# One more step between copy and use: at the projection, at a batch's turned inputs and at the router's counts

## The chip, the cores and the metric

The kernel runs on one core of one Trainium2 chip. The time is device microseconds (us) from start to end of one execution. A run's time is a median over executions; the profile is one further execution, recorded by the hardware profiler. TensorE (PE) multiplies matrices, VectorE (DVE) and ScalarE (ACT) work on elements, GpSimd (POOL) does elementwise work and indirect transfers, and SyncE (SP) issues most of the DMA transfers. Each engine, and SP's queue of transfers, takes its instructions strictly in the order in which the program wrote them: an instruction that waits holds up everything behind it on that engine.

## The reference

Input is x of shape (8, 256, 128) in float32: 8 batches of 256 tokens with 128 features. Four blocks follow each other, each with a residual and a layer normalisation:

```
x = LN(x + attention(x))      # 8 heads; a query sees its last 64 keys and 32 more,
                              # picked by an indexer's scores (top_k of 96)
x = LN(x + experts(x))        # 8 experts, each token goes to the best one, gelu
x = LN(x + recurrence(x))     # gated linear recurrence with 16 states per feature
x = LN(x + moe(x))            # sigmoid encoder, 8 experts, the best two are mixed
```

The part that matters here is the first block and the routing of the second. The indexer computes `relu(q_i k_i)` summed over 4 index heads and picks 32 past keys per query beside its own window. The keys and values of the picked positions are gathered, the 8 heads' softmax is taken over 96 keys, and the output is projected. The router takes the argmax of 8 sigmoids.

## The kernel before, in words

**Groups.** Attention is done in 128 groups (b, f, g): batch b of 8, half f of 2, and g of 8. The main loop (lines 1232 to 1265) goes through them as n = 16b + 8f + g. In iteration n the program writes the scores of group n (L710, L716 on PE, L725 on DVE), the turning of group n-2 (L746, copied by ACT in L751), the value product of group n-3 (L761), the exponentials of n (L731 on ACT), then a tick, then the reciprocal and the weights of n (L736 on DVE, L738 on ACT), then a second tick. This text calls the first tick of an iteration A and the second B. All of a group's own matmuls lie ahead of A; nothing of the groups on PE lies between A and B of one iteration.

**Sides.** Everything else is a generator in the list `sides`. At each tick every side runs from one `yield` to the next (a step), in the order in which the sides were added. So a `yield` moves all that follows in its generator by one tick, and changes whether it is written at an A or at a B. The sides here are:

- `picked(k)` (L444): the indexer of batch k, added at n = 16k - 22. Step 1 transposes x on PE through `transposed_steps` (L370), step 2 copies it on ACT (L378), step 3 has the matmuls L453 to L458, step 4 copies them out on ACT, step 6 makes the table `tab` (L478 to L480 on DVE), steps 9 to 12 find the 32 best (L519 to L523) and cast their numbers to bytes (L528, DVE), step 13 stores them to DRAM (`list`, L530, on SP's queue), and step 14 reads them back spread over the partitions (`idxb`, L535, on SP's queue). After that it does the same for the later queries (steps 14 to 22).
- `gathered(k)` (L549), in two parts: part A is added by step 14 of `picked(k)`, part B by step 22. Its first step writes the first one-hot `hot` on POOL (L560, from `idxb`); two steps later come the gathering matmuls `pgm` (L572) from that `hot`, then `pgl` a step later. POOL adds the turned keys (L589). How far a part may go is held back by the groups that still read the key buffers (L599).
- `asked(b)` (L617) makes the queries; `as_weights` (L675) copies them with 12 transfers on SP's queue (4 of L678, 8 of L680). `as_weights(b, 1)` is called at the top of iteration n = 16b + 1, ahead of its scores and its ticks.
- `projected(b, f)` (L769), added when group (b, f, 7) has had its value product, at n = 16b + 8f + 10. Step 1 transposes on DVE, step 3 on PE (L781), step 4 copies `olT` on ACT (L784), step 6 multiplies (L789). For f = 1 it goes on with the normalisation and with `routed0(b)` (L808), whose input goes through `transposed_steps` too: router matmul L817 in step 13, the one-hot of the best expert (`first_best`, L799) in step 15, the counting matmuls L835 and L836 in step 17, and in step 18 the places and two indirect transfers that POOL issues (L851).
- `response()` (L1125) computes the recurrence's response on POOL (L1150, L1168) and DVE (L1149, L1158, L1171), one POOL product every three or four ticks.
- `experts(0)` (L916) follows `routed0(5)` in the same generator; `gated(b)` (L1090), which also calls `transposed_steps`, comes after the main loop.

Which ticks these steps fall on follows from the code by counting: step s of a side that was added in iteration n0 is written at A of n0 + (s-1)/2 where s is odd, and at B of n0 + (s-2)/2 where s is even. For `picked(k)` step 14 is B of iteration 16k - 16, that is B of 16(k-1); the next thing that the program writes on SP's queue is `as_weights(k-1, 1)` at the top of iteration 16(k-1) + 1.

Of the kernel before, what the change touches and what calls it, by code (L numbers as in the profile page):

```python
# [104 lines left out]
def tile_two_layers(ctx: ExitStack, tc: tile.TileContext, a: dict, out: bass.AP):  # L105
# [8 lines left out]
    def ps(tag, name):  # L114
        return psum.tile([P, 512], F32, tag=tag, name=name, bufs={"e": 1, "x": 3}.get(tag))
# [254 lines left out]
    def transposed_steps(src, name, tag="x", copy=None):  # L370

        n = src.shape[1]
        pt = ps(tag, name + "_ps")
        for f in range(n):
            nc.tensor.transpose(pt[:, f * P : (f + 1) * P], src[:, f, :], ident)
        yield
        t = work.tile([P, 2 * P], F32, tag=f"xT{n}", name=name, bufs=4)
        (copy or nc.scalar.copy)(t[:, : n * P], pt[:, : n * P])  # L378
        yield
        return t  # L380

# [26 lines left out]
    def normalised_steps(dst, src, n, tag):  # L408

        mv = moments(src, n, tag)  # L410
        yield
        rs = work.tile([P, n], F32, tag=tag + "_rs", name=tag + "_rs")
        nc.scalar.activation(rs, mv[:, :, 1], AF.Ln, bias=eps)
        nc.scalar.activation(rs, rs, AF.Exp, scale=-0.5)
        yield
        for f in range(n):
            nc.vector.tensor_scalar(dst[:, f, :], src[:, f, :], mv[:, f, 0:1], rs[:, f : f + 1], ALU.subtract, ALU.mult)
        yield
# [25 lines left out]
    def picked(b, st):  # L444


        xb = x[:, 2 * b : 2 * b + 2, :]
        xT = yield from transposed_steps(xb, f"xT_{b}", copy=None if b else nc.vector.tensor_copy)


# [318 lines left out]
    def projected(b, f, st):  # L769

        if f == 0:
            st["x1p"] = work.tile([P, 2, D], F32, tag="x1p", name=f"x1p_{b}")
        x1p, po = st["x1p"], st["po"]

        olt = work.tile([P, NH, CKV], F32, tag="olt", name=f"olt_{b}_{f}")
        nc.vector.transpose(out=olt, in_=po[:, : TB0 * 8].rearrange("p (t h) -> p h t", h=NH))
        yield
        yield
        pt = ps("x", f"polT_{b}_{f}")
        for k in range(2):  # L780
            nc.tensor.transpose(pt[:, k * P : (k + 1) * P], olt[:, 4 * k : 4 * (k + 1), :].rearrange("p h c -> p (h c)"), ident)  # L781
        yield
        olT = work.tile([P, 2, P], F32, tag="olT", name=f"olT_{b}_{f}")
        nc.scalar.copy(olT.rearrange("p k t -> p (k t)"), pt[:, : 2 * P])  # L784
        yield
        yield
        pp = ps("o", f"pproj_{b}_{f}")
        for k in range(2):
            nc.tensor.matmul(pp[:, :D], olT[:, k, :], wuvo[:, k, :], start=k == 0, stop=k == 1)  # L789
        yield  # L790
        nc.vector.tensor_add(x1p[:, f, :], pp[:, :D], x[:, 2 * b + f, :])
        if f:
            yield
            yield from normalised_steps(x[:, 2 * b : 2 * b + 2, :], x1p, 2, "ln1")
            st["normed"] = True
            yield from routed0(b)


    def first_best(dst, val, n, top, tag):  # L799

        nc.vector.tensor_reduce(top, val, AX.X, ALU.max)
        nc.vector.tensor_tensor(dst, val, top.unsqueeze(2).to_broadcast([P, n, 8]), ALU.is_equal)
        nc.vector.tensor_mul(dst, dst, first8.unsqueeze(1).to_broadcast([P, n, 8]))
        lead = work.tile([P, n], F32, tag=tag + "_lead", name=tag + "_lead")
        nc.vector.tensor_reduce(lead, dst, AX.X, ALU.max)
        nc.vector.tensor_tensor(dst, dst, lead.unsqueeze(2).to_broadcast([P, n, 8]), ALU.is_equal)

    def routed0(b):  # L808


        k = next(k for k, (b0, nb) in enumerate(GROUPS) if b0 <= b < b0 + nb)
        ts = slice(2 * b, 2 * b + 2)
        x1T = yield from transposed_steps(x[:, ts, :], f"x1T_{b}")
        pr = ps("x", f"prt_{b}")
        for f in range(2):
            fs = slice(f * E0, (f + 1) * E0)
            nc.tensor.matmul(pr[:, fs], x1T[:, f * P : (f + 1) * P], wr, start=True, stop=True)  # L817
        yield
        rt = work.tile([P, 2, E0], F32, tag="rt", name=f"rt_{b}")
        rtf = rt.rearrange("p f e -> p (f e)")  # L820
        nc.vector.tensor_tensor(
            rt, pr[:, : 2 * E0].rearrange("p (f e) -> p f e", e=E0), br.unsqueeze(1).to_broadcast([P, 2, E0]), ALU.add
        )
        nc.scalar.activation(rtf, rtf, AF.Exp, scale=-1.0)
        yield
        nc.vector.tensor_scalar_add(rtf, rtf, 1.0)
        route = work.tile([P, 2, E0], F32, tag="route", name=f"route_{b}")
        nc.vector.reciprocal(route, rt)
        oh = onehot[:, ts, :]
        first_best(oh, route, 2, best_prob[:, ts], "moe0")  # L830
        yield
        yield
        ohf = oh.rearrange("p t e -> p (t e)")
        pc = ps("x", f"pcount_{b}")
        nc.tensor.matmul(pc[:, : 2 * E0], before, ohf, start=True, stop=True)  # L835
        nc.tensor.matmul(pc[:, 2 * E0 : 4 * E0], every, ohf, start=True, stop=True)  # L836
        yield
        rank, cnt = (pc[:, u * 2 * E0 : (u + 1) * 2 * E0].rearrange("p (t e) -> p t e", e=E0) for u in range(2))
        base, at = bases[k], work.tile([P, 2, E0], F32, tag="mat", name=f"mat_{b}")
        nc.vector.tensor_add(at[:, 0, :], base, rank[:, 0, :])  # L840
        nc.vector.tensor_add(base, base, cnt[:, 0, :])
        nc.vector.tensor_add(at[:, 1, :], base, rank[:, 1, :])
        nc.vector.tensor_add(base, base, cnt[:, 1, :])
        nc.vector.tensor_mul(at, at, oh)
        nc.vector.tensor_reduce(place[:, ts], at, AX.X, ALU.add)
        nc.vector.tensor_copy(places[:, ts], place[:, ts])  # L846
        while k not in clear:
            yield
        for f in range(2):
            t = 2 * b + f  # L850
            nc.gpsimd.indirect_dma_start(  # L851
                out=sorted_in[k][:], out_offset=bass.IndirectOffsetOnAxis(ap=places[:, t : t + 1], axis=0),
                in_=x[:, t, :], in_offset=None,
            )
        state[b]["placed"] = True
        yield
# [233 lines left out]
    def gated(b):  # L1090
        xb = x[:, 2 * b : 2 * b + 2, :]
        tag = "x" if b == B - 1 else tags["gate"]
        x2T = yield from transposed_steps(xb, f"x2T_{b}", tag=tag)
        pg = ps(tag, f"pg_{b}")
        for f in range(2):
# [136 lines left out]
    for n in range(len(groups) + 3):  # L1232
# [19 lines left out]
        if third:  # L1252
            third.latents()
            if third.g == 7:
                then = [experts(k) for k, (b0, nb) in enumerate(GROUPS) if (b0 + nb - 1, 1) == (third.b, third.f)]
                ending = chain(projected(third.b, third.f, state[third.b]), *then)
                if n < len(groups) + 2:
                    sides.append((ending, 1))
# [466 lines left out]
```

## Time and profile before

| | |
|---|---|
| median of 3 runs | 852.54 us (850.76 to 854.84) |
| the profiled execution, its own time | 855.22 us |
| its span, first to last instruction | 853.5 us |
| mean granted TensorE clock | 0.816 |
| busy: PE, DVE, POOL, ACT | 641.5, 482.9, 360.0, 324.6 us |
| groups of attention (n = 0 to 127) | from about 45 to about 617 us |
| part with the second layer's tail | from about 700 to 853 us |

A line of the timeline gives the start and the length in us, the engine, the line of the code, the operation, what it writes and reads, and how many instructions were merged; in brackets stands how long the engine sat idle before it and what ended that. SPq is SP's queue of transfers. A line of the waits gives the waiting engine and line, what it waited for, the total in us, how often, and the longest.

### The profile page before, as it was taken

Reading aid. Unit: us, or ns where it says so; the run is one execution under the profiler, and the core shown is the slowest. Engines: PE = TensorE matmul, PEld = TensorE weight load, DVE = VectorE, ACT = ScalarE, POOL = GpSimd, SP = SyncE. Lnnn points to the kernel's source line nnn. Section 1 sums busy time; section 2 is a strip of 40 time slices with the busy share of each in tenths; the row PEclk is TensorE's granted clock in tenths of the full one; section 3 lists DMA queues with packets and bytes.
Section 4 is the critical chain, followed back from the end, with each engine's and each line's share of the span. In section 5 each row is a group of like instructions: output and inputs, shape, how many; then the busy total and the mean of one; then the engine's idle time right before and its main releaser. Section 6 shows DMA issues by size and latency. Waiting matters only on the chain.

```text
span 853.5 us, 26479 instructions
## 1 busy us (share of the span) xinstructions
PE 641.5 (75%) x11019; PEld 418.8 (49%) x11019; DVE 482.9 (57%) x1792; ACT 324.6 (38%) x955; POOL 360.0 (42%) x222
## 2 busy tenths in 40 slices
PE   4477768885888897877898878787727839687973
PEld 3143434562554564454565454586616726344541
DVE  4766845679767664667665673222154345456673
ACT  3332432442343354254354444557522323322422
POOL 1454668559647735756618436000031240211110
PEclk9997677667857767898879987989877959898787
DMA  5232364210201101101101215448996540022220
GB/s 192 65 82 61 94 184 140 86 38 2 61 7 33 37 27 38 37 27 46 37 27 42 59 34 144 125 130 222 253 191 187 171 71 3 2 100 100 113 112 25
DMA packets 96192, 72.64 MB, mean 85 GB/s; under 512 B 21864, under 2 KB 86952, under 8 KB 95048
## 3 DMA queue, kind: packets, MB, share of 16 engines
q1 hardware_dynamic: 94200, 68.42, 29.3%
q0 software_dynamic: 1024, 2.10, 0.9%
q8 instruction: 87, 1.43, 0.7%
q10 hardware_dynamic: 848, 0.43, 0.2%
q14 instruction: 33, 0.27, 0.1%
HBM read 49.14 MB, written 13.91 MB: 74 GB/s over the span
## 4 chain that ended last, share of the span: by engine, by line
PE 37%; DVE 30%; ACT 12%; DMA 8%; issue 5%; POOL 4%; SPq 4%; POOLq 0%; DVEq 0%; ACTq 0%
PE pgm L572 4%; PE pe L746 4%; PE s L716 3%; PE s L710 3%; DVE cur L510 3%; PE py L1001 3%; PE pgl L572 3%; ACT sm L731 3%; PE pqr L647 2%; PE ph L986 2%; DVE hg L1608 2%; DMA w<-in_L_ffn_W_dram 2%; POOL hot L560 2%; PE pqi L453 2%; ACT eT L751 1%
## 5 line engine op out<-in xcount | busy, mean ns | idle before, releaser
L560 POOL TENSOR_SCALAR hot<-idxb,masks 128x1024 f32<-128x1024 uint8 (+2 forms) x64 | 182.1, 2851 | 107.0 <-DMA idxb<-list 65.1
L751 ACT COPY eT<-pe 128x256 f32<-128x256 f32 x128 | 47.1, 368 | 159.7 <-PE pe L746 159.3
L725 DVE CUSTOM_DVE_ANT_0 sm<-s,allowed 128x128 f32<-128x128 f32 x128 | 40.4, 316 | 114.0 <-PE s L716 104.9
L572 PE MATMUL pgm<-hot,tab 128*32 128x256 f32 (+2 forms) x1024 | 88.4, 462 | 19.3 <-POOL hot L560 18.4
L738 ACT ACTIVATE en<-sm,stat 128x128 f32<-128x128 f32 x128 | 51.4, 401 | 89.9 <-DVE stat L736 86.6
L731 ACT ACTIVATE sm<-sm,stat 128x128 f32<-128x128 f32 x128 | 51.6, 403 | 72.5 <-DVE stat L725 63.4
L851 POOL DMA_INDIRECT sorted_in<-x,places x16 | 16.3, 1017 | 125.1 <-DVE places L846 48.8
L746 PE MATMUL pe<-eye,en 128*32 128x128 f32 x1024 | 62.6, 324 | 4.5 <-ACT eT L751 4.5
L710 PE MATMUL s<-kst,qw 64*32 64x96 f32 x1024 | 58.3, 305 | 8.6 <-DVE qw L688 8.6
L572 PE MATMUL pgl<-hot,tab 128*32 128x256 f32 (+2 forms) x512 | 47.7, 460 | 20.1 <-DVE gtmp L580 8.3
L746 PE MATMUL pe<-eyes,en 128*32 128x128 f32 x1024 | 62.7, 325 | 0.0
L1467 POOL TENSOR_TENSOR ln_rs<-ln_rs,minus_half 128x4 f32<-128x4 f32 x16 | 16.3, 1020 | 104.2 <-DVE ln_rs L1466 73.9
L716 PE MATMUL s<-kg,qbd 128*32 128x32 f32 x2048 | 57.1, 236 | 0.0
L572 PEld LDWEIGHTS pgm<-hot,tab 128*32 128x32 f32 (+2 forms) x1024 | 26.9, 123 | 60.2 <-issue 29.6
L710 PEld LDWEIGHTS s<-kst,qw 64*32 64x32 f32 x1024 | 28.2, 141 | 51.6 <-issue 39.6
L716 PEld LDWEIGHTS s<-kg,qbd 128*32 128x32 f32 x2048 | 41.7, 147 | 22.8 <-issue 13.7
L589 POOL TENSOR_TENSOR kg<-gtmp 128x256 f32<-128x256 f32 x48 | 35.8, 749 | 30.6 <-DVE gtmp L580 27.9
L588 DVE STREAM_TRANSPOSE rows<-pgl 128x256 f32<-128x256 f32 x48 | 21.5, 447 | 47.3 <-ACT kg L587 47.3
L580 DVE TENSOR_TENSOR gtmp<-pgm,cg 128x512 f32<-128x512 f32 x48 | 32.4, 676 | 19.8 <-PE pgm L572 19.7
L1001 PE MATMUL py<-w,hT 128*128 128x128 f32 x240 | 35.6, 309 | 10.1 <-ACT hT L992 7.9
L736 DVE RECIPROCAL stat<-stat 128x1 f32<-128x1 f32 x128 | 19.4, 152 | 39.5 <-ACT sm L731 38.0
L761 PEld LDWEIGHTS pav<-eT,win 96*32 96x32 f32 x1024 | 37.7, 134 | 2.9 <-issue 0.8
(298 smaller groups left out, 1490.4 us busy)
## 6 DMA issues: line engine op xcount, KB each, us to landing
w<-in_L_ffn_W_dram SPq DMA_DIRECT2D x60, 256.0 KB
sorted_in<-zero SPq DMA_DIRECT2D x34, 256.0 KB
toep<-kpad SPq DMA_DIRECT2D x32, 256.0 KB
gb<-gates SPq DMA_DIRECT2D x8, 1024.0 KB
idxb<-list SPq DMA_DIRECT2D x16, 256.0 KB
qbd<-qd SPq DMA_DIRECT2D x60, 64.0 KB
qw<-qd SPq DMA_DIRECT2D x120, 32.0 KB
mxs<-sorted_in SPq DMA_DIRECT2D x30, 64.0 KB
```

Of the source, the lines that this page charges most:

```text
L560: nc.gpsimd.tensor_scalar(out=t[:m].rearrange("p j g k -> p j (g k)"), in0=st["listed", u][:m].rearrange("p (j g) k -> p j g k", j=2)[:, : ...
L572: nc.tensor.matmul(pt[DR * i : DR * (i + 1), :], tab[:m, k, c, :], t[:m, :, i, :], start=k == 0, stop=k == len(hot) - 1,)
L589: nc.gpsimd.tensor_tensor(kgf[:, 0], t1[:, 0], t1[:, 1], ALU.add)
L710: nc.tensor.matmul(s[TB0 * j : TB0 * (j + 1), :WIN], qws[f][:, :, :, 8 * j + g].rearrange("p i h -> p (i h)"), st["kst"][:, TB0 * w : TB0 ...
L716: nc.tensor.matmul(s[TB0 * j : TB0 * (j + 1), WIN:KEYS], qbds[f][:, k, :, :, 8 * j + g].rearrange("p i h -> p (i h)"), kg[:, 1 - k, :], st ...
L725: nc.vector.tensor_tensor_reduce(out=self.sm, in0=s[:, :KEYS], in1=allowed[f][:, g * KEYS : (g + 1) * KEYS], scale=-SCALE, scalar=3.0e38, ...
L731: nc.scalar.activation(self.sm, self.sm, AF.Exp, bias=self.stat[:, 0:1], scale=-1.0, accum_out=self.stat[:, 1:2])
L738: nc.scalar.activation(self.en, self.sm, AF.Copy, scale=self.stat[:, 2:3])
L746: nc.tensor.matmul(pe[rows, k * P : (k + 1) * P], self.en[:, WIN:KEYS] if k else self.en[:, rows], own_rows[i] if k else ident, start=True ...
L751: nc.scalar.copy(self.eT.rearrange("p k t -> p (k t)"), pe[:, 0 : 2 * P])
L761: nc.tensor.matmul(st["po"][js, TB0 * g : TB0 * (g + 1)], rows if k else st["win"][:, w, :], self.eT[: P if k else WIN, k, js], start=k == ...
L1001: nc.tensor.matmul(py[:, u * D : (u + 1) * D], hT[u][:, c, :], w2[:, c, :], start=c == 0, stop=c == FFN0 // P - 1)
```

## The change

Three `yield`s are added, and nothing else: no instruction is added or removed.

```diff
@@ transposed_steps (called by picked, routed0 and gated) @@
         (copy or nc.scalar.copy)(t[:, : n * P], pt[:, : n * P])
         yield
+        yield
         return t
@@ projected @@
         nc.scalar.copy(olT.rearrange("p k t -> p (k t)"), pt[:, : 2 * P])
         yield
         yield
+        yield
         pp = ps("o", f"pproj_{b}_{f}")
@@ routed0 @@
         first_best(oh, route, 2, best_prob[:, ts], "moe0")
+        yield
         yield
         yield
         ohf = oh.rearrange("p t e -> p (t e)")
```

So in `picked(k)` all that stands behind the copy of step 2 is written one tick later, which turns each A into a B and each B into an A of the next iteration; `gathered(k)` is added one tick later with it. In `projected` the product L789 moves from step 6 to step 7. For f = 1 the router's matmul comes two ticks later than before, and the counts, the places and the indirect transfers three ticks later. `experts(0)` starts three ticks later. In `gated` what follows the copy comes one step later.

## The prediction, made before the changed kernel was run

> **What bounds the kernel now.** I read the page first, then the waits of PE, then the timeline of SP's queue, POOL and PE around each moved step. The page's chain gives no single owner:
>
> ```profile
> PE 37%; DVE 30%; ACT 12%; DMA 8%; issue 5%; POOL 4%; SPq 4%; POOLq 0%; DVEq 0%; ACTq 0%
> ```
>
> In the groups' stretch PE is the nearest to a bound: from 450 to 500 us it is busy 41.8 of 50, DVE 30.4, ACT 23.4, POOL 27.9. PE runs strictly in order and its waits are many and short, so a time is won by taking waits from PE and lost by giving it new ones. The waits of PE over the whole span:
>
> ```profile
> PE pgm L572 <- POOL hot L560: 18.4, 10, 4.7
> PE pqi L453 <- ACT xT L378: 10.7, 7, 2.9
> PE pproj L789 <- ACT olT L784: 9.1, 7, 1.7
> PE pcount L835 <- DVE onehot L806: 5.3, 3, 2.1
> ```
>
> The last three are what the extra steps stand in front of, 25.1 us together. (prt after x1T and pg after x2T wait 0.5 us each.) The first is the one to watch: the gather's matmuls follow right behind POOL's one-hot, which follows right behind a transfer. SP's queue, POOL and PE in batch 7's turn, from the timelines of those engines:
>
> ```profile
> 466.36 0.48 SPq L530 DMA_DIRECT2D list<-idxs  x1
> 468.11 0.32 SPq L535 DMA_DIRECT2D idxb<-list  x1
> 468.55 0.64 SPq L678 DMA_DIRECT2D qbd<-qd  x1
> 469.23 1.83 SPq L680 DMA_DIRECT2D qw<-qd  x2
> ...
> 476.40 1.23 SPq L680 DMA_DIRECT2D qw<-qd  x2
> ```
> ```profile
> 471.68 2.84 POOL L560 TENSOR_SCALAR hot<-idxb,masks 96x1024 f32<-96x1024 uint8 x1 [2.96 <-DVE stat L736]
> ```
> ```profile
> 471.89 2.34 PE L572 MATMUL pgm<-hot,tab 128*32 128x256 f32 x32
> 474.57 1.07 PE L572 MATMUL pgm<-hot,tab 96*32 96x256 f32 x16 [0.35 <-POOL hot L560]
> 475.97 1.21 PE L572 MATMUL pgl<-hot,tab 128*32 128x256 f32 x16 [0.32 <-DVE rows L588]
> ```
>
> The reader sees that idxb goes out one place ahead of twelve qbd and qw transfers that hold SP's queue until 477.6; that hot starts 3.6 us after idxb; and that PE takes hot 0.05 us after its end, having waited 0.35. There is no slack at all.
>
> **Part 1: the turned inputs of picked(k), and SP's queue.** The step that issues idxb moves from B of iteration 16(k-1) to A of the next one, so past the top of that iteration, where as_weights writes its 12 transfers. From then on idxb stands behind them. Nothing makes them wait (qbd follows idxb at once), so they are a plain delay of SP's queue. The new end of hot is: list, plus the block of twelve (list's own issue is 0.5), plus about 3.0 from idxb's issue to the start of hot (213.41 to 216.36, 411.14 to 414.12), plus 2.84 of hot, 6.4 us with list's 0.5 and the seam. list itself comes one tick later, behind one group's L725 and a transpose on DVE: I take 1.5 us, and 0 for batch 3, whose cast L528 lost 3.1 us beside POOL (3.26 against 0.18 elsewhere) and need not again. For the batches 3 to 7:
>
> - batch 3: list 211.70 + block 8.9 + 6.4 = 227.0; pgm stood at about 221.6 (last third of the run of 48 from 218.57 to 223.1): 5.4 late
> - batch 4: 278.29 + 1.5 + 9.1 + 6.4 = 295.3 against 288.83: 6.4
> - batch 5: 344.91 + 1.5 + 8.8 + 6.4 = 361.6 against 354.76: 6.8
> - batch 6: 409.42 + 1.5 + 8.3 + 6.4 = 425.6 against about 418.1: 7.5
> - batch 7: 466.36 + 1.5 + 9.1 + 6.4 = 483.4 against 474.57: 8.8
>
> Sum 34.9. pgm is itself written one tick later, so one pgl of 16 (1.2 us) now runs ahead of it: minus 6.0. While PE waits, DVE works off what it lags (at 418 to 422 it has 4 us queued, part of which PE would have waited for): 1 us each, minus 5. Leaves 24. Batch 2 had POOL busy until 140.1, its hot moves hardly: 0.5. Batch 1 passes no such block. Who waits behind: on PE the scores of the next group, and through them DVE's L725 and ACT's L731; on POOL the key sums and the response's products behind hot. Bounds: 15 if PE's later waits take most of it back, 35 if none. I take 24.5.
>
> The Trainium skill (DMA: Bandwidth & Descriptors, Rules for kernel authors) says to issue a transfer early and to wait on it late, since the fixed set-up cost then overlaps. By that alone, an issue one step later costs one step at most, 1.5 us less what is hidden, some 5 us for five batches. The rows say otherwise: what is late is not the set-up (list to idxb 1.7 us) but the place in the queue (8.3 to 9.1 us). I go by the rows.
>
> **Part 2: routed0, and POOL's queue.** The two indirect transfers come three ticks later. On POOL stand behind them the one-hots of the next part B:
>
> ```profile
> 448.88 1.06 POOL L851 DMA_INDIRECT sorted_in<-x,places  x1 [13.36 <-DVE stat L725]
> 451.59 0.96 POOL L851 DMA_INDIRECT sorted_in<-x,places  x1 [1.65 <-DMA sorted_in<-x,places]
> 452.59 8.74 POOL L560 TENSOR_SCALAR hot<-idxb,masks 128x1024 f32<-128x1024 uint8 x3
> ```
>
> PE takes the first two of them at 459.29, 1.0 us after their end (452.59 + 5.65 = 458.24). Three ticks are one and a half groups: the places would come after L725 at 452.96 instead of ahead of the one at 448.50, so some 5 to 6 us later, and PE waits up to 5 us. In batch 5's turn (L851 at 388.86, PE at 400.40) 3 to 4, in batch 3's (255.80, and the response's product can go ahead) 2 to 3, batch 4's hots waited for L1168 anyway and batch 2's have more room: 0 to 1, batch 7's 0 to 2. Sum about 12; DVE lags here too, so I take 8, with bounds 0 and 14.
>
> **Part 3: what the steps take away.** At the projection: five of the seven waits are those of f = 1 (1.72, 1.09, 1.72, 1.72, 1.72), where ACT's copy stands behind DVE's search. With one more step a whole group's matmuls come in between, so the wait at this place goes. But all five lie 8 to 10 us behind the new wait of part 1, in which DVE catches up, so they would shrink anyway: of 9.1 I take 5. At the turned inputs the copy is at B and its use at A; one more step puts the use at B, ahead of the same group as before. Only another side's matmuls come in between (polT, 0.4 to 0.7): of 10.7 I take 2. At the counts the one-hot is written at A and used at A; moved by three, A to B, one group lies between as before: of 5.3 I take 1. Sum 8, bounds 3 and 25. In late steps (gated after the groups) the generators run with nothing in between, and a yield has no time of its own: 0. Parity also swaps ACT's five copies of L461 to L473 (about 1.7 us) from behind en to ahead of it; en is used two groups later: 0.
>
> **Part 4: the clock.** The stretches table of before, around a PE wait of 4.15 us at 209:
>
> ```profile
> 209.00:213.00 4.00, 0.14 (x4) 0.00 (x0) 3.18 (x4) 0.75 (x3) 4.00 (x3) 1.00 0.02 5
> ...
> 216.00:219.00 3.00, 3.00 (x92) 2.30 (x84) 2.42 (x7) 2.18 (x7) 2.64 (x1) 0.50 0.26 63
> 219.00:222.00 3.00, 3.00 (x32) 0.56 (x24) 2.11 (x8) 0.75 (x3) 0.89 (x2) 0.62 0.18 44
> ```
>
> After the idle time the granted clock (third from the right) is 0.50 for some microseconds. The groups there take 1.94 us from one to the next (214.82 to 216.76) against 1.26 at full clock (469.33 to 470.59), and the gathers 6.3 against 5.3: some 2.4 us in all. The Trainium skill (TensorE: Matmul & The Clock Gate, What's actually happening) says that an idle window of about 3.4 us halves the clock until a busy window: by that each of five new waits costs 2.4, 12 us. By the rows less: batches 3 and 6 already run these matmuls partly at a lower clock, and after 422 us PE is busy only 2.35 of 4 us, so slow matmuls fit into its gaps. I take 4, bounds 0 and 12.
>
> **Part 5: DVE beside POOL.** Some DVE steps take much longer while POOL works: L478 4.75 us at 262.19 against 0.23 at 328.99, L528 3.26 against 0.18, L510 5.93 against 0.31. All of them move by a tick, some into a POOL operation and some out of one. The trace can't say which: 0, bounds -6 and +6.
>
> **Sum.** 24.5 + 8 - 8 + 4 + 0 = 28.5 us. Against the profiled execution: span 853.5 + 28.5 = 882.0, with the 1.7 around it 883.7. The median of before is 2.7 below its 855.22, so 881.0.
>
> **The rivals.**
> - *Slower, as summed (chance 0.74)*: 881, own range 864 to 898. For it: the order on SP's queue is fixed by the code, and in batches 4, 5 and 7 PE takes hot 0.05 us after its end (1.1 us in batch 6, some 2.4 in batch 3).
> - *Slower by more (0.12)*: part 1 in full (35), part 2 in full (14), the clock at 12, gains 5: 56, so 909. For it: PE is the nearest to a bound. Against: DVE's lag behind PE, which waits absorb.
> - *Nothing to speak of (0.05)*: the new waits are taken back by those they replace, 15 + 0 - 15 = 0, so 852. The change then does little of what it says: at two of its three places no group's matmuls come between copy and use.
> - *Faster (0.09)*: the three waits of 25.1 us go as a whole, and idxb's delay stays hidden: about 835 to 845. The point from which this decides is the room between the end of hot and pgm. With 9 us of it SP's block costs nothing. The rows show 0.05 us in batch 7; it would have to come from PE being so much later by other waits that these would cost the same.
>
> **Numbers.** Faster by over 0.5% (under 848.3) 0.09, within 0.5% 0.05, slower 0.86; 0.5% is about what a measurement here can tell from no change. The range 858 to 900 leaves out the faster case and most of the slower-by-more one.
>
> **What would show it.** In the changed profile idxb L535 of batches 3 to 7 stands behind qw L680 and not ahead of qbd L678; hot starts about 12 us after list instead of 5; PE pgm from POOL hot rises from 18.4 to 40 us or more, and pproj from olT falls below 3. L851 lies 5 us later against its group, and a second pgm wait per batch follows it. Part 1 is wrong if hot of a batch's first part still starts before the last qw; part 2 if the two-hot pgm doesn't wait. If the time is under 860, PE got back elsewhere what it lost there.

## The result, and the profile after

The changed kernel takes 947.8 us (median of 4 runs, 946.4 to 949.8) against 853.7 us (850.8 to 861.2) for the kernel before, run beside it: a ratio of 1.109 with a 95% interval of 1.101 to 1.116. That is 94 us slower. The forecast was 28 us slower, and its range ended at 900. Executions that took over 1.5% more than the fastest of their kernel are left out of the ratios: two of four of run 6, seven of twelve of run 10 (all twelve together have a median of 858.4), one of ten of run 14 and a few of the kernel before.

The chain of work that ended last now holds more transfers, POOL and SP's queue, where PE and DVE were:

```profile
PE 34%; DVE 23%; DMA 13%; ACT 9%; POOL 8%; SPq 8%; issue 5%; POOLq 0%; DVEq 0%; ACTq 0%
```

The waits of PE in the changed kernel (total, times, longest, in us), and two of before that the prediction does not show:

```profile
PE pgm L573 <- POOL hot L561: 102.7, 22, 10.0
...
PE x1T_ps L375 <- DVE x L418: 15.4, 7, 3.7
PE polT L782 <- DVE stat L737: 14.8, 7, 4.1
...
PE pe L747 <- ACT eT L752: 10.1, 8, 4.4
...
PE pcount L838 <- DVE onehot L808: 2.2, 1, 2.2
```
```profile
PE pe L746 <- ACT eT L751: 4.5, 6, 1.7
...
PE x1T_ps L375 <- DVE x L417: 1.9, 1, 1.9
```

Three things are to be seen. The waits that the steps were put in front of are gone: pqi on ACT's xT fell from 10.7 to 0.3, pproj on olT from 9.1 to 0.5, pcount from 5.3 to 2.2. The wait of pgm for the one-hots rose by 84 us. And three waits came that the prediction does not name: x1T on the norm (1.9 before), polT on DVE (1.1 before) and pe (4.5 before).

Batch 6's turn in the changed kernel, first SP's queue, then POOL and PE, from the timelines (the prediction shows batch 7's of before; batch 7's of now, with its list at 542.79, looks the same):

```profile
468.05 0.48 SPq L531 DMA_DIRECT2D list<-idxs  x1
468.62 0.64 SPq L679 DMA_DIRECT2D qbd<-qd  x1
...
476.23 1.23 SPq L681 DMA_DIRECT2D qw<-qd  x2
477.56 0.52 SPq L536 DMA_DIRECT2D idxb<-list  x1
```
```profile
480.80 2.84 POOL L561 TENSOR_SCALAR hot<-idxb,masks 96x1024 f32<-96x1024 uint8 x1 [11.09 <-DMA idxb<-list]
```
```profile
483.69 1.93 PE L573 MATMUL pgm<-hot,tab 96*32 96x256 f32 x16 [9.52 <-POOL hot L561]
```

idxb now goes out behind the twelve transfers, 9.5 us after list; in this batch it was 1.7 before. The one-hot starts 12.75 us after list instead of 4.7, and PE, which was at pgm at 474.2, waits 9.5 us. All six batches from 2 to 7 look like this (8.7 to 10.0 us each, 56.5 us together; 3.2 us before).

The second part of a batch, on POOL and on PE (this is batch 5's; the prediction shows batch 6's of before, which happens to stand at nearly the same time):

```profile
448.20 1.06 POOL L854 DMA_INDIRECT sorted_in<-x,places  x1 [10.38 <-DVE stat L737]
452.32 0.96 POOL L854 DMA_INDIRECT sorted_in<-x,places  x1 [3.06 <-DMA sorted_in<-x,places]
453.32 8.50 POOL L561 TENSOR_SCALAR hot<-idxb,masks 128x1024 f32<-128x1024 uint8 x3
```
```profile
456.23 1.08 PE L573 MATMUL pgm<-hot,tab 128*32 128x256 f32 x8 [2.77 <-POOL hot L561]
459.06 3.10 PE L573 MATMUL pgm<-hot,tab 64*32 64x256 f32 x24 [1.74 <-POOL hot L561]
```

The pair of indirect transfers and the three one-hots stand in the same order as in the prediction's row, but PE now comes to the first of the two one-hots 2.8 us before its end, and pays 1.74 more for the second. The waits of this second part are 32.0 us over the six batches; before they were 5.0, all in one batch.

The stretches table, before and after, over the groups of attention and nothing else (columns: stretch, its length, PE busy, weight load, DVE, ACT, POOL, then granted clock, DMA share, GB/s):

```profile
45.00:622.00 577.00, 466.59 (x9426) 305.11 (x9426) 335.41 (x1201) 243.54 (x773) 295.08 (x161) 0.80 0.29 77
```
```profile
42.00:715.00 673.00, 481.52 (x9410) 311.74 (x9410) 319.85 (x1201) 241.29 (x773) 297.06 (x162) 0.74 0.26 67
```

So the groups take 96 us more and the tail behind them takes nothing more (231 and 230 us). Of the 96 us, 81 are idle time of PE (577.0 - 466.6 = 110.4 before, 191.5 after), and 15 are the same matmuls taking longer at a lower granted clock. The 84 us that pgm gained stand for all of the idle time; the waits lost and the waits newly found nearly cancel.

### The profile page after: what moved, and what is told of

Same layout as the page of the kernel before. It is cut to its first block, busy times and chain, and to the rows that moved or that the text cites. A ratio compares the mean times of both kernels' runs of the same rounds, so it can differ in the third digit from the quotient of the medians.

```text
span 945.9 us, 26476 instructions
## 1 busy us (share of the span) xinstructions
PE 655.1 (69%) x11019; PEld 426.0 (45%) x11019; DVE 465.7 (49%) x1792; ACT 322.5 (34%) x955; POOL 360.0 (38%) x222
## 4 chain that ended last, share of the span: by engine, by line
PE 34%; DVE 23%; DMA 13%; ACT 9%; POOL 8%; SPq 8%; issue 5%; POOLq 0%; DVEq 0%; ACTq 0%
POOL hot L561 6%; SPq L681 5%; PE pgm L573 4%; PE pe L747 4%; DMA w<-in_L_ffn_W_dram 4%; DMA idxb<-list 3%; PE s L717 3%; PE s L711 3%; PE py L1004 3%; PE ph L989 2%; DVE hg L1611 2%; PE pqr L648 2%; SPq L679 2%; PE pgl L573 2%; DMA gb<-gates 1%
## 5 line engine op out<-in xcount | busy, mean ns | idle before, releaser
L573 PE MATMUL pgm<-hot,tab 128*32 128x256 f32 (+2 forms) x1024 | 92.6, 478 | 105.3 <-POOL hot L561 102.7
L726 DVE CUSTOM_DVE_ANT_0 sm<-s,allowed 128x128 f32<-128x128 f32 x128 | 36.5, 285 | 187.4 <-PE s L717 187.3
L747 PE MATMUL pe<-eye,en 128*32 128x128 f32 x1024 | 65.8, 339 | 10.1 <-ACT eT L752 10.1
L747 PE MATMUL pe<-eyes,en 128*32 128x128 f32 x1024 | 65.7, 338 | 0.0
L589 DVE STREAM_TRANSPOSE rows<-pgl 128x256 f32<-128x256 f32 x48 | 21.5, 447 | 48.6 <-ACT kg L588 48.4
L590 POOL TENSOR_TENSOR kg<-gtmp 128x256 f32<-128x256 f32 x48 | 34.9, 732 | 22.9 <-DVE gtmp L581 20.3
L1004 PE MATMUL py<-w,hT 128*128 128x128 f32 x240 | 36.4, 315 | 10.2 <-ACT hT L995 8.4
L989 PE MATMUL ph<-mxsT,w 128*128 128x128 f32 x240 | 34.0, 293 | 12.1 <-DMA w<-in_L_ffn_W_dram 11.5
L747 PEld LDWEIGHTS pe<-eyes,en 128*32 128x32 f32 x1024 | 39.5, 140 | 2.4
```

Source lines behind the costliest of these rows:

```text
L573: nc.tensor.matmul(pt[DR * i : DR * (i + 1), :], tab[:m, k, c, :], t[:m, :, i, :], start=k == 0, stop=k == len(hot) - 1,)
L726: nc.vector.tensor_tensor_reduce(out=self.sm, in0=s[:, :KEYS], in1=allowed[f][:, g * KEYS : (g + 1) * KEYS], scale=-SCALE, scalar=3.0e38, ...
L747: nc.tensor.matmul(pe[rows, k * P : (k + 1) * P], self.en[:, WIN:KEYS] if k else self.en[:, rows], own_rows[i] if k else ident, start=True ...
L989: nc.tensor.matmul(ph[u][:, cs_], w1[:, cs_], xsT[:, u * P : (u + 1) * P], start=True, stop=True)
L1004: nc.tensor.matmul(py[:, u * D : (u + 1) * D], hT[u][:, c, :], w2[:, c, :], start=c == 0, stop=c == FFN0 // P - 1)
```

## The experiments

The theory after this look was: two queues, SP's and POOL's, each hold the one-hots back. The rivals were that one queue does it all, or that the steps themselves do it by where they put an instruction in its group. Every time below stands beside runs of the kernel before on the same chip, whose median was 852.9, 859.8, 852.9 and 850.8 us in the four sets.

### 1 and 2: the two halves of the change

Edit of run 1, and in run 2 the same switch at x1T with the steps at the projection and the counts:

```
-    def transposed_steps(src, name, tag="x", copy=None):
+    def transposed_steps(src, name, tag="x", copy=None, late=False):
...
         yield
+        if late:
+            yield
...
+        xT = ... transposed_steps(xb, f"xT_{b}", copy=..., late=True)
```

> The kernel before with the extra step after the copy in picked alone; projection, router inputs, counts and gates are as before. Theory (place in SP's queue): the first index transfer of batches 2 to 7 goes out behind the twelve transfers of as_weights, its one-hots come late, and each such batch keeps the 9 to 10 us wait of the changed kernel in front of the first part's pgm (56.5 us there over six batches, 3.2 before). Then about 905 us, and pgm waits for hot some 65 to 75 us in all. Rival (POOL's queue behind the indirect transfers does it): these are not moved here, so under 865. Rival (the places add up to more than their parts): between, and the parts' sum would stay far from 94.

> The kernel before with the extra steps at the projection, after the copy of routed0 and in front of the counts; picked and the gates are as before. The indirect transfers then come three ticks later, and idxb keeps its place ahead of the twelve transfers. Theory: only the second part's pgm waits longer (in the changed kernel some 32 us over six batches against about 5), less what pproj and pcount give back (9 and 3): 865 to 875 us. Rival (POOL's queue does most of it): 900 or more. Rival (clock and DVE): no new pgm wait, but a time over 870 all the same.

Run 1 took 903.8 us (ratio 1.059, 1.051 to 1.066), 50.9 more than before. Run 2 took 901.1 us (1.059, 1.053 to 1.064), 48.2 more. Together that is 99 us against the 94 of the whole change: within the intervals the two add up, and nothing is left for x2T in the gates. Run 1 came out as expected. Run 2 did not: 870 were expected, and its time is the one that the rival named (900 or more, POOL's queue). The wait of PE for hot in run 1 and in run 2:

```profile
PE pgm L574 <- POOL hot L562: 68.7, 12, 9.0
```
```profile
PE pgm L574 <- POOL hot L562: 46.6, 19, 5.6
```

In run 2 pgm waits 28 us more than before, about as the theory has it (27), so the rival's reason does not hold for the whole of it; but the run is 48 us slower. Some 20 us were unexplained.

### 3 and 4: SP's queue alone

Run 3 is the changed kernel with this edit; run 4 is the kernel before with as_weights called between the two ticks of the group ahead, so that the twelve transfers come between list and idxb with no extra step anywhere:

```
-            if (f, g) == (0, 1):
+            if (f, g) == (0, 2):
                 as_weights(state[b], 1)
```

> The changed kernel, but as_weights for f = 1 is called one group later, at g = 2, so that its twelve transfers stand behind idxb again; nothing else differs. Theory: the first part's waits of 9 to 10 us go, the second part's stay: about 890 to 900 us, pgm waits for hot 45 to 55 us instead of 102.7. Rival (POOL's queue): stays over 930. Rival (the extra step itself brings hot too near its use, whatever the queue): hot still ends behind PE's arrival by 1 us or more in each batch, and the time stays over 915.

> The kernel before with no extra step; as_weights for f = 1 is called half a group earlier, between the two ticks of g = 0, so that its twelve transfers stand between list and idxb as in the changed kernel. Theory: the first part's pgm waits some 8 to 9 us in each of the batches 2 to 7 with no other change, so 890 to 905 us. Rival (the extra steps matter by themselves, not through this queue): within 10 us of the kernel before.

Run 3: 901.5 us (1.059, 1.054 to 1.064), so 45.5 of the 94 us are gone, and pgm waits 52.8 instead of 102.7. Run 4: 896.3 us (1.054, 1.049 to 1.060), 43.4 us lost by the block's place alone. Run 3 lies 1.5 us above its expectation. Run 4's time lies within its own, though each of its new waits is 5.0 to 7.5 us and not 8 to 9, and batch 2's hardly rose. The place of idxb behind twelve transfers costs 43 to 46 us, with or without the extra steps.

### 5: POOL's queue

Run 2's kernel, with the indirect transfers of batches 0 to 4 and 6 written ten steps later (the expectation names only 0 to 4, but the edit leaves out 5 and 7 alone):

```
+        for _ in range(0 if b in (5, 7) else 10):
+            yield
         for f in range(2):
             t = 2 * b + f
```

> The second run (extra steps at projection, routed0 and counts) with the indirect transfers of batches 0 to 4 written another ten steps later, so that on POOL they stand behind the one-hots of the second part and ahead of those of the next first part; batches 5 and 7 stay. Theory (half of the 48 us is the second part's pgm waiting on one-hots that stand behind the pair of indirect transfers on POOL, 27 us over six batches, the other half the turned halves of a group: x1T behind the norm, pqi, pe, some 21): pgm waits of the second part go in five of six batches, about 875 to 882 us. Rival (POOL's order is no matter, the waits come from the steps' halves alone): within 8 us of the second run's 901. Rival (POOL's order is all of it): under 862.

It took 895.8 us (1.044, 1.038 to 1.050), 36.0 more than before where run 2 had 48.2. That is 12 us back, where the theory had 20 to 26. (The raw time is within the first rival's 8 us of 901, but the kernel before was 7 us slower in this set.) The timelines of POOL and PE show why:

```profile
288.13 1.06 POOL L857 DMA_INDIRECT sorted_in<-x,places  x1 [0.16 <-issue]
290.75 0.96 POOL L857 DMA_INDIRECT sorted_in<-x,places  x1 [1.56 <-DMA sorted_in<-x,places]
291.75 2.86 POOL L562 TENSOR_SCALAR hot<-idxb,masks 96x1024 f32<-96x1024 uint8 x1
```
```profile
294.66 1.94 PE L574 MATMUL pgm<-hot,tab 96*32 96x256 f32 x16 [6.38 <-POOL hot L562]
```

The pair is out of the second part's way, but now it stands directly ahead of the next batch's first one-hot (96 rows), and PE waits 6.4 us there. Over the batches 2 to 7 the second part's waits fell from 31 us to 7, and the first part's rose from 6 to 17. The experiment moved the cost as well as taking it; it needed a better place (run 13).

### 6, 7 and 8: the router's three steps, one at a time

One more yield at the projection (6), after the copy of x1T (7), in front of the counts (8), each alone in the kernel before.

> The kernel before with the extra step at the projection alone. Theory: pproj's 9 us of waits go, but all later steps of the chain change their half of the group: the norm now ends at the first half and x1T is turned at once, which waits some 16 us as in the second run; the indirect transfers come one step later, some 5 us in pgm. So 862 to 870 us. Rival (pproj's wait is a gain without a price): 840 to 848.

> The kernel before with the extra step after the copy in routed0 alone. The norm keeps its half, prt, counts and places change theirs, the indirect transfers come one step later. Theory: some 5 to 10 us in pgm of the second part, x1T and pproj as before: 855 to 865 us. Rival (POOL's order decides): 870 or more. Rival (no effect): 850 to 855.

> The kernel before with the extra step in front of the counts alone. The indirect transfers come one step later as in the run before this one, and only pcount and what follows change their half: pcount's 5 us may go. Theory: 850 to 862 us. Rival (POOL's order decides): 870 or more, the same as the run before this one.

All three took longer than expected: run 6 took 873.0 and 882.5 us, about 18 over its 859.8; run 7 876.7 us (1.025, 1.017 to 1.033), 16.9 over; run 8 872.3 us (1.020, 1.011 to 1.029), 12.4 over. (The kernel before was 7 us slower in this set. Measured from it, run 6 is at the upper end of what was expected, the other two a little above.) No single one of them moved pgm's wait by more than 3 us in all, so the one-hots behind POOL's queue are not what a single step costs, although runs 7 and 8 took the time that this rival named. Their sum of 47 us meets the 48 of run 2 by chance: run 2 has 28 us of pgm's waits that they lack. And they have something that run 2 lacks: behind the groups, PE is idle for 82 to 83 us where it was 78 before, and waits 5.4 to 6.1 us once, ahead of the last polT, for which the profile names no cause. Run 6's other waits are:

```profile
PE x1T_ps L375 <- DVE x L417: 15.0, 9, 2.9
PE pcount L836 <- DVE onehot L807: 13.0, 5, 6.0
```

These places have no extra step in run 6; they only come one step later. The timelines of DVE and PE show what that does, in the kernel before:

```profile
370.11 0.12 DVE L736 RECIPROCAL stat<-stat 128x1 f32<-128x1 f32 x1
...
370.74 0.59 DVE L417 TENSOR_SCALAR x<-x1p,ln_mv,ln_rs 128x128 f32<-128x128 f32 x2
```
```profile
373.29 0.44 PE L375 MATMUL x1T_ps<-eye,x 128*128 128x128 f32 x2
```

and in run 6:

```profile
380.45 1.52 DVE L417 TENSOR_SCALAR x<-x1p,ln_mv,ln_rs 128x128 f32<-128x128 f32 x2
381.89 0.15 DVE L736 RECIPROCAL stat<-stat 128x1 f32<-128x1 f32 x1
```
```profile
381.44 0.30 PE L375 MATMUL x1T_ps<-eye,x 128*128 128x128 f32 x1 [2.36 <-DVE x L417]
```

The reciprocal L736 marks the seam between a group's two steps. Before, the norm L417 is written behind it, in the group's second step; x1T follows in the next group's first step, and between the two PE has that group's scores, pe and pav to do. In run 6 the norm is written ahead of the seam and x1T right behind it: PE has nothing of its own in between and waits 2.4 us. Of these, 0.9 are the norm itself, which took 1.52 us instead of 0.59; in three batches in which it took 0.56, x1T waits 1.7 to 1.8 all the same. One group has two steps that are not alike. A single extra step puts everything behind it into the other one.

### 9: the same step, twice

If that is so, two extra steps at the projection should be cheaper than one.

> The kernel before with two extra steps at the projection and none elsewhere. A group has two steps, so the norm, x1T, prt, counts and places stay in their half and only come a group later; the indirect transfers come two steps later. Theory of the halves: pproj's 9 us go, x1T and pcount wait no more than before (the single extra step gave them 13 and 8 us more), the second part's pgm pays 5 to 15: 850 to 865 us. Rival (each step later costs by its place, the half is no matter): as much as or more than the single step's 25 us, 875 or more.

It took 860.9 us (1.010, 1.007 to 1.013): 8.0 us over before, where the single step has 18. x1T waits 5.8 us instead of 15.0 and pcount 7.6 instead of 13.0, though both come later still; they don't quite fall to the 1.9 and 5.3 of before, as they were expected to.

### 10, 11 and 12: the indirect transfers in POOL's gap

The loop of run 5 with more steps, so that the pair stands behind the next batch's first part, where POOL is idle: in the kernel before (10), with the two steps at the projection (11), and in the changed kernel with the block of run 3 moved as well (12).

> The kernel before with the indirect transfers of batches 0 to 4 written 18 steps later, where POOL has a gap between the last one-hot of one first part and the next second part; no other step moves. Theory of POOL's queue: the 5 us that pgm waits for two one-hots in batch 5 go, nothing comes in their place: 843 to 853 us. Rival (their place is no matter): within 3 us of before.

> The two extra steps at the projection together with the late indirect transfers. Theory of both: pproj's wait goes and POOL's queue costs nothing: 838 to 848 us, faster than before. Rival: the wait that pproj gives up comes back at the next of PE's waits, 850 or more.

> The changed kernel with as_weights of f = 1 one group later and with the indirect transfers of batches 0 to 4 written 15 steps later, so both queues are out of the way. Theory: of 94 us some 50 go with SP's queue and some 20 with POOL's; what stays are x1T, polT and pe, with their part of the clock: 870 to 880 us. Rival (the steps' halves are most of the second half): 890 or more. Rival (the two queues are all): under 860.

Run 10: ratio 1.001 (0.996 to 1.006), no difference that can be told, and so on the rival's side; the 5 us in one batch stayed (2.78 and 2.17), so it is not the pair that causes them. Run 11: 847.0 us (0.994, 0.990 to 0.998), the only version that beats both kernels, the one before by about 5 us: no half changes, no queue is hit, and no wait for olT is left in PE's list. It is 14 us faster than run 9, but not by the one-hots: pgm waits 25.6 us here and 26.2 there. Run 12: 877.7 us (1.027, 1.022 to 1.033), as expected. With both queues mended, 25 of the 94 us stay; pgm still waits 12 us more than before.

### 13 to 16: halves against queue

Run 2's single steps with the pair in POOL's gap (13); each of the router's three steps doubled with the pair in the gap (14) and with the pair left to come six steps later (15); and run 1 with the block of run 3 (16).

> The second run (single extra steps at the projection, routed0 and counts, 48 us over before) with the indirect transfers of batches 0 to 4 written 15 steps later, in POOL's gap behind the next first part, where they stand ahead of no one-hot that is waited for (in the fifth run they stood ahead of one, and 12 us of new first-part waits took the place of the second part's). Theory: 20 to 25 us less than the second run, 873 to 882 us; what stays is from the steps' halves. Rival (halves are nothing): under 862. Rival (POOL's queue is nothing): over 893.

> The same with each of the three extra steps doubled (two at the projection, two after the copy in routed0, two in front of the counts) and the indirect transfers of batches 0 to 4 at the same place of POOL's gap. All steps keep their half of the group and come one, two and three groups later. Theory of the halves: x1T, pe and polT wait no more than before: 842 to 858 us, some 20 us under the run before this one although every step comes later. Rival (lateness by itself costs): 875 or more.

> The doubled steps of the run before this one, the indirect transfers not moved further, so that they come six steps later than in the kernel before. Theory: the second part's one-hots stand behind them or just ahead of them; if behind, pgm pays as in the second run or more, 20 to 35 us: 870 to 888 us. If six steps already carry them past the two one-hots, the time is near the run before this one. Rival (halves and lateness both nothing): 848 to 858.

> The first run (the extra step in picked alone, 51 us over before) with as_weights for f = 1 one group later, so that idxb stands ahead of the twelve transfers again. Theory (SP's queue is all that the extra step in picked costs, and pqi's 9 us are given back): 843 to 858 us, and the first part's pgm waits under 10 us in all. Rival (hot comes too near its use by the step itself): 870 or more.

| router's steps | pair in its place | pair in POOL's gap |
|---|---|---|
| single | +48.2 us (run 2) | +30.8 us (run 13), ratio 1.031 (1.023 to 1.040) |
| doubled | +28.9 us (run 15), ratio 1.029 (1.020 to 1.038) | +0.9 us (run 14), ratio 1.001 (0.997 to 1.006) |

Across the table POOL's queue costs 17 and 28 us; down it, the half costs 19 and 30. Taken from the ratios, which are formed in another way than the differences of medians, the four places are +50, +26, +25 and +1 us, so 24 for the queue and 24 to 25 for the half in both lines: that the two add up is as good a reading as that they don't. Every step of run 14 comes later than in run 13, and yet it is some 25 to 30 us faster. Lateness by itself costs nothing here, with one exception: in the runs 5 and 10 to 14 batch 6's pair moved too and lands behind the groups. PE is idle there for 82 to 84 us instead of 78 (in the runs 10 to 14 it waits 17 us for sorted_in and less elsewhere), so 4 to 6 us of their times stand there, and the pair's place in the other batches is worth as much more. The waits of run 13, and then of run 14, at the two places in question:

```profile
PE pgm L574 <- POOL hot L562: 26.5, 14, 4.1
...
PE x1T_ps L375 <- DVE x L419: 19.1, 9, 2.9
```
```profile
PE pgm L575 <- POOL hot L563: 30.3, 16, 4.2
...
PE x1T_ps L375 <- DVE x L420: 9.9, 8, 3.1
```

pgm is no less in run 14, so what parts them is not the one-hots; x1T halves, and pqi goes from 21.5 to 13.0 us. Over all of PE's waits run 14 has 197 us, as the kernel before, and run 13 221. One thing was expected otherwise: x1T and pe wait more in run 14 than before (9.9 and 14.6 us against 1.9 and 4.5), and it is pproj and others that give it back. In run 15 pgm waits 53.7. The times of all four lie within what the theory expected of them. Run 16 took 857.0 us (1.005, 1.001 to 1.009), 6.2 over before: the step in picked costs 45 us by SP's queue and 6 by anything else. Whether a doubled step in picked would be cheaper still was not tried.

## Why the prediction was wrong in size

The sign and the first two mechanisms were right; three of its five terms were too small, and a fourth had the wrong sign.

| part of the prediction | predicted | measured |
|---|---|---|
| 1, idxb behind the twelve transfers | +24.5 | 43 to 46 (runs 3, 4, 1 less 16) |
| 2, one-hots behind the indirect pair | +8 | 17 to 28 (runs 2, 13, 14, 15), 24 (run 3 less 12) |
| 3, waits that the steps take away (and 5, DVE beside POOL, 0) | -8 | +19 to +30 (runs 2, 13 to 15), 25 at most (run 12) |
| 4, clock | +4 | about 15, contained in the above |
| sum | +28.5 | +94 |

**Part 1.** The end of hot was forecast to within 0.9 us, and mostly 0.3: list plus 15.3, 15.5, 15.2, 14.7 and 15.5 for the batches 3 to 7; the trace has 15.55, 15.28, 14.72, 15.59 and 15.68. What failed is what was taken off behind that: "minus 6.0" for the pgl that runs ahead, "minus 5" for DVE's backlog, and "its hot moves hardly: 0.5" for batch 2. PE did not come to pgm later, it came sooner. Before, PE was there 10.2, 9.6 and 7.9 us after list in the batches 4, 5 and 7, where it has a row of its own; in the changed kernel 5.8 to 6.8 us after, in every batch from 2 on.

Run 4, in which list and pgm keep their steps, has PE there 9.0 to 10.2 us after list in the batches 3 to 7 and waits of 6.0, 7.5, 6.8, 6.3 and 5.0, sum 31.5: close to the prediction's gross sum of 34.9 (and batch 2's wait rises by 0.6 there, as forecast). In run 1, which has the step in picked, PE is there 6.5 to 7.7 us after list, and the six waits are 50.8 us. The groups' stretch in run 4 and then in run 1:

```profile
44.67:657.81 613.14, 478.51 (x9426) 312.44 (x9426) 332.69 (x1201) 244.01 (x773) 294.97 (x161) 0.76 0.28 72
41.76:668.36 626.60, 475.89 (x9426) 307.09 (x9426) 324.02 (x1201) 241.72 (x773) 296.25 (x162) 0.76 0.28 72
```

In run 4 PE's idle time rose by 24 us, which is what the prediction left; what it lacks there is the clock, since the same matmuls took 12 us longer. (The profiled execution of run 4, 891.1 us, is 36 us over that of before, and so a little faster than its median.) In run 1 the idle time rose by 40 us and the busy time by 9: PE came sooner instead of later, so that the six waits grew by 47.6 us, 12 more than the gross sum with batch 2's 0.5, where 11 had been taken off it. That PE comes earlier there is likely the half of the group again, but was not tried by itself.

**Part 2.** The mechanism and the place were named, and the pair did come some 6 us later against the part's first pgm, in the two turns that were looked at. Of the six turns in which a pair stands ahead of two one-hots, four came out near the prediction's figures: the turn at 322.61 rose by 1.1 us (0 to 1 forecast), the one at 388.86 to 4.5 (3 to 4), at 448.88 to 4.2 (up to 5), at 505.62 to 2.2 (0 to 2). The first two made the difference: the turn at 182.05 waits 7.7 us (0 to 1, "more room") and the one at 255.80 7.4 (2 to 3). The first of them on POOL and on PE, before and then in the changed kernel:

```profile
186.05 5.65 POOL L1150 TENSOR_TENSOR tmp<-pow 128x1024 f32<-128x1024 f32 x2
191.68 2.85 POOL L560 TENSOR_SCALAR hot<-idxb,masks 128x1024 f32<-128x1024 uint8 x1
```
```profile
195.42 1.08 PE L572 MATMUL pgl<-hot,tab 128*32 128x256 f32 x8 [3.58 <-ACT isc L504]
...
198.23 2.07 PE L572 MATMUL pgm<-hot,tab 128*32 128x256 f32 x16
```
```profile
203.44 2.78 POOL L1153 TENSOR_TENSOR tmp<-pow 128x1024 f32<-128x1024 f32 x1
206.20 2.85 POOL L561 TENSOR_SCALAR hot<-idxb,masks 128x1024 f32<-128x1024 uint8 x1
```
```profile
209.10 1.08 PE L573 MATMUL pgm<-hot,tab 128*32 128x256 f32 x8 [5.92 <-POOL hot L561]
```

Before, the one-hot was ready at 194.5 and PE came for it at 198.2. Now it is ready at 209.0, and PE has been there since 203.2. Half of that is POOL's: the one-hots, which started 0.9 and 1.3 us after the part's first pgm in these two turns, start 5.7 and 5.5 after it. The pair comes later, and its second transfer waits longer for the first to land (3.6 and 3.2 us where it was 1.8 and 2.3); one of the response's two products that stood behind it before stands elsewhere now, which gives 2.8 us back. The other half is PE's: it reached this pgm 7.4 and 7.8 us after the part's first one, of which 3.6 and 4.0 were a wait for ACT (the row of pgl), and now reaches it 2.7 us after. The room that the prediction counted on was in part a wait of PE itself, and that wait is gone. Besides, the 12 that the prediction found were cut to 8 for DVE's lag, for which it shows no row. Single steps moved pgm by under 3 us in all (runs 6 to 8), the three together by 28; that the first steps use up a slack fits this, but was not tried further.

**Part 3 is the failed step.** It lists what the extra steps take away and asks of each place only what lies between its copy and its use. The waits that it names did go, by more than the 8 us it took (22.1 of 25.1). But an extra step in a chain moves everything behind it too, and with an odd number into the other half of a group. The prediction looked at that for five copies on ACT and for DVE beside POOL, and put 0 for both. The norm and x1T, which stand directly behind the projection in the same chain, were not looked at, nor pcount and polT. With the same steps doubled, this loss is gone (run 14 against run 13, run 15 against run 2): what costs is an odd number of steps, and not that they come later.

**Part 4.** The term was too small by two factors: there are some twelve new waits for the one-hots of 2 us and more and not five, and each was dearer. The prediction took 0.8 us for each, since "slow matmuls fit into its gaps"; the rule of the Trainium skill that it set beside the rows (TensorE: Matmul & The Clock Gate, What's actually happening) gave 2.4. Measured are 15 us over twelve, 1.3 each if they are shared out evenly, between the two. After the wait of 9.5 us shown above, in batch 6, PE's clock (third column from the right) is at half again:

```profile
483.60:487.00 3.40, 3.31 (x56) 1.70 (x60) 0.30 (x2) 0.00 (x0) 3.40 (x3) 0.50 0.00 0
```

PE is busy 3.31 of 3.40 us here: there are no gaps for slow matmuls to fit into, because the wait has piled up work.

**The rivals.** "Slower by more" had the right direction, but even with the parts 1, 2 and 4 at their upper bounds it kept gains of 5 us in part 3 and came to 909. "Faster" named its deciding point rightly, the room between the end of hot and pgm; there was none. Of the signs that the prediction named, idxb behind qw, hot 12 us after list, pgm above 40 and pproj below 3 are all in the trace.

What stays open: what runs 6 to 8 wait for ahead of the last polT, and the rest of run 8's 12 us, of which its waits show no single owner (pgm, pgl, pe, pqi and pcount rose by 1.5 to 4.4 us each); what causes the 5 us that stayed in run 10; why pqi waits 21 us in runs 2 and 13, where no step of picked was moved; what gives run 11 its 14 us over run 9. And three steps at one place, odd but later than two, were not tried: that the further steps of runs 9 and 14 help by the slack they give, and not by being even in number, is therefore not excluded; the rows of x1T in run 6 speak for the number.

## What to carry to other kernels

When a generator of steps is woven into a loop with two unlike seams, an extra step is not a delay: ask for everything behind it in its chain, and not only for the place it was put, which seam it lands in and what each in-order engine has between producer and consumer there; if slack is wanted, add it in whole rounds of the loop (two steps cost 8 us where one cost 18, and with the indirect transfers moved as well won 5). Ask of each transfer that moves which block of transfers it passes on its queue: here one place cost 45 us through an instruction two engines away. And do not subtract from a new wait what might absorb it without a row that shows it, nor count a wait of the engine itself as room for another.

## What the runs showed of the hardware that was not expected

The second indirect transfer of a pair waits on POOL until the first has landed (3.06 us in the changed kernel's row above, 1.56 in run 5's), with the one-hots behind it held up for as long; whether the chip asks for that or only this program's dependency between the two writes was not tried. And a wait of PE is worth more than its length: in run 4 24 us of added idle time came with 12 us of slower matmuls (granted clock 0.76 over the groups, 0.80 before), in the whole change 81 with 15 (0.74).
